# Six rows per partition set aside by SyncE instead of four, and the table's first parts fetched in between

## The chip, the cores and the metric

The kernel runs on one core of a Trainium2 chip. A core has engines that run side by side, each with its own instruction stream: TensorE (matrix products and transposes), VectorE, ScalarE, GpSimd and SyncE, and 16 DMA engines that move data between HBM and the on-chip memory (SBUF). SyncE does no arithmetic: it starts transfers. The metric is the device time in microseconds (us) from the start to the end of one execution; the median of three timed executions is given. The profile is of one further execution.

## The reference

1024 sequences of 50 item numbers each look up rows of an embedding table of 100001 rows with 128 numbers (row 0 counts as zeros). Running sums over the sequence are divided by a length, normalized over the batch, and fed through a recurrence over the 50 positions that counts threshold crossings ("spikes"). The counts times the whole table give the scores.

```python
emb = emb_table.at[0].set(0.0)
e = emb[seq]                                   # 1024 x 50 x 128
prefix = jnp.cumsum(e, axis=1)
denom = jnp.minimum(t_idx[None, :], lengths[:, None]).astype(e.dtype)
uF = prefix / denom[:, :, None]
mean = uF.mean(axis=0)
var = uF.var(axis=0)
y = (uF - mean) * lax.rsqrt(var + BN_EPS) * gamma + beta
x_seq = jnp.moveaxis(y, 1, 0)

def step(v, x):                                # TAU = 2, V_TH = 1
    v = v + (x - v) / TAU
    spike = atan_spike(v - V_TH)               # 1 where v >= V_TH
    v = v - lax.stop_gradient(spike) * V_TH
    return (v, spike)
_, spikes = lax.scan(step, v0, x_seq)
uF_out = spikes.mean(axis=0)                   # 1024 x 128
scores = uF_out @ emb.T                        # 1024 x 100001
```

The scores are 409.6 MB of float32, which have to be written to HBM.

## The kernel before

There are two stages. In the first, each of the T = 50 steps needs the embedding rows of all 1024 sequences at one position: 8 blocks (n = 0 to 7) of 128 rows, one row per partition. GpSimd brings a block with one indirect transfer (a gather). TensorE transposes the blocks and adds them up in PSUM (`pre`), in two halves of 512 sequences; VectorE scales each half into `uF` and takes its statistics, and does the recurrence with ScalarE. In the second stage the counts are multiplied with the table, part by part (a part is 1024 rows, 0.5 MB), and the scores are stored.

SyncE starts the loads: first the inputs, then the first 36 parts of the table in six groups of six, one large transfer a group (`rows` tiles, 3 MB each). Then it fetches some single rows of the table by itself, so that GpSimd has fewer gathers: block 0 of steps 44 to 47. For each partition it loads four item numbers into registers and starts four transfers of one row (512 bytes). Gathers of the other blocks stay with GpSimd. At the end of the first stage SyncE starts the stores of the scores.

```python
        for g in range(AHEAD):                          # AHEAD = 6 groups
            fetch(group(g), g * GROUP, GROUP)           # GROUP = 6 parts

        aside = {}
        for t0, many in ((T - 6, 4),):
            for t in range(t0, t0 + many):
                aside[t] = once.tile([P, P], F32, tag=f"aside{t}", name=f"aside_{t}")
            for p in range(P):
                _, items = nc.values_load_multi_w_load_instructions(
                    idx[p : p + 1, 0, t0 : t0 + many], engines=[mybir.EngineType.SP], ...)
                for j, item in enumerate(items):
                    nc.sync.dma_start(out=aside[t0 + j][p : p + 1, :], in_=table[bass.ds(item, 1), :])

        def gather(t):
            es[t] = gp.tile([P, B], F32, tag="e", name=f"e_{t}")      # two buffers
            for n in range(t in aside, NB):                           # NB = 8
                nc.gpsimd.indirect_dma_start(out=es[t][:, n * P : (n + 1) * P], in_=table, ...)
        ...
        for t in range(T):
            last = t == T - 1
            if t + 1 < T:
                gather(t + 1)
            e = es.pop(t)
            if last:
                s = ...(v >= V_TH)                      # the spikes of step 48, ahead of step 49
                nc.vector.tensor_tensor(negv, s, v, ALU.subtract)
            for h, cs in enumerate(halves):
                for k in range(0, BANK, P):             # BANK = 512
                    nc.tensor.matmul(                   # a transpose, added to pre
                        pre[h][:, k : k + P],
                        lhsT=aside[t] if h == k == 0 and t in aside else e[:, h * BANK + k : ...],
                        rhs=ident, is_transpose=True, ...)
                nc.vector.scalar_tensor_tensor(uF[:, cs], rlen[:, cs], 1.0 / (t + 1), pre[h], ...)
                nc.vector.bn_stats(bs[:, h, :], uF[:, cs])
            ...                                         # statistics, spikes of step t - 1, the new v
            if t in (T - 8, T - 6):                     # two parts of the table made ready
                prepare(q, ...)
```

(... marks cuts.) `prepare` transposes a part of the table and splits it into two summands; those of parts 0 and 1 are done in steps 42 and 44, the others in the second stage. There, stores go out on SyncE's queue, and further parts of the table are fetched on ScalarE's.

Of the kernel before, what the change touches and what calls it, by code (L numbers as in the profile page):

```python
# [12 lines left out]
F32 = mybir.dt.float32  # L13
BF16 = mybir.dt.bfloat16
F32R = mybir.dt.float32r
I32 = mybir.dt.int32
# [4 lines left out]
P = 128  # L21
# [4 lines left out]
BANK = 512  # L26
GROUP = 6
AHEAD = 6

WIDTHS = [2, 2, 2, 3, 3, 3, 3] + 12 * [6] + [4, 4]  # L30
NARROW, MIDDLE = 3, 7


@with_exitstack
def rec_kernel(
# [9 lines left out]
    nc = tc.nc  # L45
    B, T = seq.shape
    N, D = table.shape
    NB = B // P
# [22 lines left out]
    parts = -(-N // HALF)  # L71
    assert sum(WIDTHS) == parts
    rows = {}
# [6 lines left out]
    def size(q):  # L80
        return min(HALF, N - q * HALF)

    def group(g):
        at = g if g < AHEAD else AHEAD - 2 + g % 2
        r = rowp.tile([P, GROUP, HALF], F32, tag=f"rows{at}", name=f"rows_{g}")
        for k in range(GROUP):
            rows[g * GROUP + k] = r[:, k, :]
        return r

    def fetch(r, q, n):  # L90

        engine = nc.sync if q < AHEAD * GROUP else nc.scalar
        k = q % GROUP
        n = min(n, parts - q)
        whole = n - (size(q + n - 1) < HALF)
        if whole:
            engine.dma_start(
                out=r[:, k : k + whole, :],
                in_=table[q * HALF : (q + whole) * HALF, :].rearrange("(q p k) d -> p q (k d)", p=P, k=KQ),
            )  # L100
        if whole < n:
            full, rest = divmod(size(parts - 1), P)
            c1 = (parts - 1) * HALF
            r = r[:, k + whole, :].rearrange("p (k d) -> p k d", d=D)
            if full:
                engine.dma_start(
                    out=r[:, :full, :],
                    in_=table[c1 : c1 + full * P, :].rearrange("(k p) d -> p k d", p=P),
                )
            if rest:  # L110
                engine.dma_start(out=r[:rest, full, :], in_=table[c1 + full * P : N, :])
# [49 lines left out]
    with ExitStack() as ph:  # L161
        once = ph.enter_context(tc.tile_pool(name="once", bufs=1))
# [7 lines left out]
        idx = once.tile([P, NB, T], I32, tag="idx", name="idx")  # L170
# [5 lines left out]
        gb = once.tile([P, 2], F32, tag="gb", name="gb")  # L176
        nc.sync.dma_start(out=gb[:, 0:1], in_=gamma.rearrange("(d o) -> d o", o=1))
        nc.sync.dma_start(out=gb[:, 1:2], in_=beta.rearrange("(d o) -> d o", o=1))
        for g in range(AHEAD):
            fetch(group(g), g * GROUP, GROUP)  # L180

        aside = {}
        for t0, many in ((T - 6, 4),):
            for t in range(t0, t0 + many):
                aside[t] = once.tile([P, P], F32, tag=f"aside{t}", name=f"aside_{t}")
            for p in range(P):
                _, items = nc.values_load_multi_w_load_instructions(
                    idx[p : p + 1, 0, t0 : t0 + many],  # L190
                    engines=[mybir.EngineType.SP],
                    min_val=0,
                    max_val=N - 1,
                    skip_runtime_bounds_check_because="items are rows of the table; the transfer checks its own bounds",
                )
                for j, item in enumerate(items):
                    nc.sync.dma_start(out=aside[t0 + j][p : p + 1, :], in_=table[bass.ds(item, 1), :])

        es = {}

        def gather(t):
            es[t] = gp.tile([P, B], F32, tag="e", name=f"e_{t}")
            for n in range(t in aside, NB):
                nc.gpsimd.indirect_dma_start(  # L204
                    out=es[t][:, n * P : (n + 1) * P],
                    out_offset=None,
                    in_=table,
                    in_offset=bass.IndirectOffsetOnAxis(ap=idx[:, n, t : t + 1].bitcast(U32), axis=0),
                )

        make_identity(nc, ident)
        gather(0)


# [53 lines left out]
        def correct(t, l):  # L268
            for h in range(B // BANK):
                nc.tensor.matmul(  # L270
                    pre[h],
                    lhsT=l,
                    rhs=zT[:, h * BANK : (h + 1) * BANK],
                    start=t == 0,
                    stop=False,
                    skip_group_check=True,
                )
# [22 lines left out]
# [6 lines that stand above are left out]
                s = lp.tile([P, B], BF16, tag="s", name=f"s_{t - 1}")  # L306
                nc.vector.tensor_single_scalar(s, v, V_TH, ALU.is_ge)
                nc.vector.tensor_tensor(negv, s, v, ALU.subtract)
            uF = up.tile([P, B], F32, tag="uF", name=f"uF_{t}")
            bs = sp.tile([P, B // BANK, 6], F32, tag="bs", name=f"bs_{t}")  # L310
            for h, cs in enumerate(halves):
                for k in range(0, BANK, P):
                    nc.tensor.matmul(  # L313
                        pre[h][:, k : k + P],
                        lhsT=aside[t] if h == k == 0 and t in aside else e[:, h * BANK + k : h * BANK + k + P],
                        rhs=ident,
                        start=False,
                        stop=last,
                        is_transpose=True,
                        skip_group_check=True,  # L320
                    )
                nc.vector.scalar_tensor_tensor(uF[:, cs], rlen[:, cs], 1.0 / (t + 1), pre[h], ALU.max, ALU.mult)  # L322
                nc.vector.bn_stats(bs[:, h, :], uF[:, cs])  # L323
            if not last:
                correct(t + 1, l)
            else:

                counted(t - 1, s)
                count = once.tile([P, B], F32, tag="zT", name="count")
                for h, cs in enumerate(halves):  # L330
                    nc.scalar.copy(count[:, cs], sums[h])
            mv = sp.tile([P, 2], F32, tag="mv", name=f"mv_{t}")
            nc.vector.bn_aggr(mv, bs.rearrange("p h s -> p (h s)"))  # L333


            r = sp.tile([P, 1], F32, tag="r", name=f"r_{t}")
            nc.scalar.activation(r, mv[:, 1:2], AF.Sqrt, bias=eps)  # L337
            nc.scalar.activation(uF, uF, AF.Identity, bias=mv[:, 0:1], scale=-1.0)


            if t and not last:
                s = lp.tile([P, B], BF16, tag="s", name=f"s_{t - 1}")
                nc.vector.tensor_single_scalar(s, v, V_TH, ALU.is_ge)  # L343
                counted(t - 1, s)

            nc.vector.reciprocal(r, r)
            q = sp.tile([P, 1], F32, tag="q", name=f"q_{t}")
            nc.vector.tensor_mul(q, r, r)
            nc.vector.scalar_tensor_tensor(q, mv[:, 1:2], BN_EPS, q, ALU.add, ALU.mult)
            nc.vector.tensor_scalar(q, q, -0.5, 1.5, ALU.mult, ALU.add)  # L350
            a = sp.tile([P, 1], F32, tag="a", name=f"a_{t}")
            nc.vector.tensor_scalar(a, q, r, hgb[:, 0:1], ALU.mult, ALU.mult)  # L352


            def x(vt, cs):
                nc.scalar.activation(vt, uF[:, cs], AF.Identity, bias=hgb[:, 1:2], scale=a)  # L356

            def step(vt, cs):
                nc.vector.scalar_tensor_tensor(vt, negv[:, cs], -0.5, vt, ALU.mult, ALU.add)

            if not last:
                vt = vp.tile([P, B], F32, tag=f"v{t % 2}", name=f"v_{t}")
                x(vt, whole)
                if t:
                    nc.vector.tensor_tensor(negv, s, v, ALU.subtract)
                step(vt, whole)
                v = vt
                if t + 2 < T:
                    l = only(t + 2)

                if t in (T - 8, T - 6):
                    q = (t - T + 8) // 2
                    prepare(q, vp.tile([P, HALF], F32, tag="v1", name=f"pt_{q}"))
# [45 lines left out]
    q0 = 0  # L419
    to_split = WIDTHS[0]  # L420
    to_fetch = AHEAD * GROUP
# [4 lines left out]

    for c, W in enumerate(WIDTHS):

# [17 lines left out]
        q1 = q0 + W  # L446
        q2 = q1 + (WIDTHS[c + 1] if c + 1 < len(WIDTHS) else 0)

# [9 lines left out]
        for n in range(NB):  # L458
            if c == 0 and n == 0:
                continue  # L460
            pool, tag, most = turns[blocks % len(turns)]
# [23 lines left out]
            if n in (1, 4) and c >= MIDDLE and to_fetch < parts:  # L485
                g = to_fetch // GROUP
                if to_fetch % GROUP or to_split >= (g - 1) * GROUP:
                    if to_fetch % GROUP == 0:
                        r = group(g)
# [23 lines left out]
```

## Time and profile before

| | |
|---|---|
| time, median of 3 executions | 1776.19 us (1770.98 to 1776.4) |
| span of the profiled execution | 1569.9 us |
| GpSimd | 374.6 us busy, 402 instructions |
| VectorE | 940.7 us busy, 1161 instructions |
| TensorE (matrix products) | 1153.1 us busy, 4548 instructions |
| ScalarE | 630.6 us busy, 700 instructions |
| HBM read / written | 77.69 MB / 409.60 MB |

The profiled execution was about 205 us shorter than the timed ones; its inner times are used as they are.

In the profile, a row of slices cuts the span into 40 equal pieces, and a digit is the busy share in tenths. The chain of waits goes back from the last instruction to what released each step. A group of instructions is given with its line of the program, engine, operation, written and read tiles, count, then busy us and mean ns of one, then the idle time ahead of them and what ended it. PE and PEld are TensorE's products and weight loads, DVE is VectorE, ACT is ScalarE, POOL is GpSimd, SPq is SyncE's queue. The time shown for an instruction that starts a transfer is that of the start, not of the transfer.

### The profile page before, as it was taken

The numbers are of one execution on the slowest core, as the hardware profiler recorded it, in microseconds if no ns is written. First come the engines' busy times: TensorE is split into PE (matmuls) and PEld (weight loads), VectorE is DVE, ScalarE is ACT, GpSimd is POOL, SyncE is SP. The second block draws the span as 40 slices with busy tenths as digits, with TensorE's granted clock in tenths as the row PEclk, the third lists the DMA queues.
The fourth block names the chain that finished last, engine by engine and source line by source line (L and its number), as shares of the span: only waits on it lengthen the run. The fifth ranks groups of instructions, "written<-read, shape, count | busy, mean of one in ns | idle before, by whom it ended". The sixth has DMA issues, their size and how long they took to land.

```text
span 1569.9 us, 14231 instructions
## 1 busy us (share of the span) xinstructions
PE 1153.1 (73%) x4548; PEld 822.3 (52%) x4548; DVE 940.7 (60%) x1161; ACT 630.6 (40%) x700; POOL 374.6 (24%) x402
## 2 busy tenths in 40 slices
PE   4555555555556988899878788887788888788784
PEld 2222222222233766677666666666666666666563
DVE  4777777777778665576545555555555545555453
ACT  2322222222233554465444444444444444444342
POOL 6777777777775000000000000000000000000000
PEclk7555555555555999999999988999999998989998
DMA  9622222222222999999999999999999999999998
GB/s 342 245 55 53 55 54 54 54 53 54 52 53 64 399 411 420 420 393 428 425 432 427 429 428 424 418 422 424 428 413 420 415 424 429 421 423 409 394 423 354
DMA packets 54600, 488.25 MB, mean 311 GB/s; under 512 B 12443, under 2 KB 13756, under 8 KB 33276
## 3 DMA queue, kind: packets, MB, share of 16 engines
q1 hardware_dynamic: 33008, 429.03, 65.1%
q0 software_dynamic: 12672, 25.98, 6.2%
q10 hardware_dynamic: 8844, 32.33, 5.2%
q8 instruction: 36, 0.59, 0.1%
q14 instruction: 40, 0.33, 0.1%
HBM read 77.69 MB, written 409.60 MB: 310 GB/s over the span
## 4 chain that ended last, share of the span: by engine, by line
DMA 52%; POOL 17%; PE 11%; issue 9%; ACT 5%; DVE 4%; DVEq 0%; ACTq 0%; SPq 0%; POOLq 0%
DMA scores<-o 49%; POOL e L204 17%; PE po L149 9%; ACT o L473 5%; DMA e<-in_L_rec_emb_table,idx 3%; DVE o L471 2%; PE pt L119 1%; DVE bs L323 1%; DVE uF L322 0%; DVE s L343 0%; PE pre L313 0%; PE sums L281 0%; DMA idx<-in_r_seq 0%; ACT hi L141 0%; ACT pairs L141 0%
## 5 line engine op out<-in xcount | busy, mean ns | idle before, releaser
L471 DVE TENSOR_SCALAR o<-po 128x1024 f32<-128x1024 f32 x391 | 463.5, 1220 | 351.8 <-DMA scores<-o 323.4
L473 ACT ACTIVATE o<-po 128x1024 f32<-128x1024 f32 (+1 forms) x391 | 387.9, 1018 | 547.8 <-DMA scores<-o 344.9
L204 POOL DMA_INDIRECT e<-in_L_rec_emb_table,idx x396 | 373.9, 944 | 123.4 <-issue 114.6
L149 PE MATMUL po<-pairs,countB 128*128 128x512 f32 x1168 | 314.7, 415 | 67.6 <-ACT o L473 50.7
L149 PEld LDWEIGHTS po<-pairs,countB 128*128 128x128 f32 x1168 | 225.8, 198 | 132.5 <-ACT o L473 65.8
L149 PE MATMUL po<-pairs,countC 128*128 128x512 f32 x876 | 239.1, 419 | 43.6 <-ACT o L473 43.6
L313 PE MATMUL pre<-ident,e 128*128 128x128 f32 x396 | 153.1, 450 | 143.8 <-DMA e<-in_L_rec_emb_table,idx 142.2
L149 PEld LDWEIGHTS po<-pairs,countC 128*128 128x128 f32 x876 | 170.1, 200 | 89.7 <-ACT o L473 54.7
L313 PEld LDWEIGHTS pre<-ident,e 128*128 128x128 f32 x396 | 78.5, 201 | 236.1 <-DMA e<-in_L_rec_emb_table,idx 214.7
L142 DVE TENSOR_TENSOR pairs<-pt,pairs 128x1024 fp32r<-128x1024 f32 (+1 forms) x73 | 88.3, 1217 | 96.6 <-ACT pairs L141 96.5
L337 ACT ACTIVATE r<-mv,eps 128x1 f32<-128x1 f32 x50 | 14.7, 295 | 300.6 <-DVE mv L333 300.6
L322 DVE SCALAR_TENSOR_TENSOR uF<-rlen,pre 128x512 f32<-128x512 f32 x100 | 68.3, 683 | 103.8 <-PE pre L313 103.8
L119 PE MATMUL pt<-ident,rows 128*128 128x128 f32 x782 | 113.5, 293 | 8.0 <-ACT o L473 3.9
L119 PEld LDWEIGHTS pt<-ident,rows 128*128 128x128 f32 x782 | 102.6, 154 | 28.8 <-issue 10.0
L149 PE MATMUL po<-hi,countB 128*128 128x512 f32 x200 | 82.8, 414 | 18.8 <-ACT o L473 13.8
L281 PE MATMUL sums<-s,ident_h 128*128 128x512 bf16 x98 | 49.6, 608 | 60.6 <-DVE s L343 60.6
L270 PE MATMUL pre<-zT,l 128*128 128x512 f32 x100 | 78.0, 782 | 21.6 <-DVE uF L322 21.5
L149 PE MATMUL po<-lo,countB 128*128 128x512 f32 x200 | 80.4, 402 | 0.0
L141 ACT CAST pairs<-pt 128x1024 fp32r<-128x1024 f32 (+1 forms) x73 | 73.6, 1008 | 16.2 <-PE pt L119 15.9
L149 PE MATMUL po<-pairs,countA 128*128 128x512 f32 (+1 forms) x292 | 73.2, 393 | 9.1 <-ACT o L473 9.1
L149 PE MATMUL po<-hi,countC 128*128 128x512 f32 x150 | 62.7, 418 | 16.4 <-ACT o L473 16.4
L356 ACT ACTIVATE v<-uF,hgb,a 128x1024 f32<-128x1024 f32 x49 | 59.2, 1208 | 37.4 <-DVE a L352 37.4
(78 smaller groups left out, 821.1 us busy)
## 6 DMA issues: line engine op xcount, KB each, us to landing
scores<-o SPq DMA_DIRECT2D x96, 3072.0 KB
scores<-o SPq DMA_DIRECT2D x32, 1536.0 KB
rows<-in_L_rec_emb_table ACTq DMA_DIRECT2D x20, 1536.0 KB
scores<-o SPq DMA_DIRECT2D x22, 1024.0 KB
rows<-in_L_rec_emb_table SPq DMA_DIRECT2D x6, 3072.0 KB
scores<-o SPq DMA_DIRECT2D x8, 2048.0 KB
scores<-o SPq DMA_DIRECT2D x8, 1872.5 KB
aside<-in_L_rec_emb_table SPq DMA_DIRECT2D x512, 0.5 KB
```

Of the source, the lines that this page charges most:

```text
L119: nc.tensor.transpose(pt[:, k0 : k0 + kw], r[:kw, k0 : k0 + D], ident[:kw, :kw])
L141: nc.scalar.copy(vh, vp)
L142: nc.vector.tensor_tensor(vl, vp, vh.bitcast(F32), ALU.subtract)
L149: nc.tensor.matmul(po[:, :kw], lhsT=counts[n], rhs=part[:, k0 : k0 + kw], start=j == 0, stop=j == 1,)
L204: nc.gpsimd.indirect_dma_start(out=es[t][:, n * P : (n + 1) * P], out_offset=None, in_=table, in_offset=bass.IndirectOffsetOnAxis(ap=idx[: ...
L270: nc.tensor.matmul(pre[h], lhsT=l, rhs=zT[:, h * BANK : (h + 1) * BANK], start=t == 0, stop=False, skip_group_check=True,)
L281: nc.tensor.matmul(sums[h], lhsT=ident_h, rhs=s[:, h * BANK : (h + 1) * BANK], start=t == 0, stop=t == T - 2, skip_group_check=True,)
L313: nc.tensor.matmul(pre[h][:, k : k + P], lhsT=aside[t] if h == k == 0 and t in aside else e[:, h * BANK + k : h * BANK + k + P], rhs=ident ...
L322: nc.vector.scalar_tensor_tensor(uF[:, cs], rlen[:, cs], 1.0 / (t + 1), pre[h], ALU.max, ALU.mult)
L356: nc.scalar.activation(vt, uF[:, cs], AF.Identity, bias=hgb[:, 1:2], scale=a)
L471: nc.vector.tensor_scalar_mul(o[:, h0 : h0 + hw], po[:, :hw], 1.0 / T)
L473: nc.scalar.mul(o[:, h0 : h0 + hw], po[:, :hw], 1.0 / T)
```

## The change

SyncE takes over six blocks in place of four: blocks 6 and 7 of steps 46, 47 and 48, in place of block 0 of steps 44 to 47. It is to relieve GpSimd of two further gathers. To begin with the rows early, only the first group of the table's parts is fetched ahead of them; the other 30 parts are fetched one at a time, one after every fourth partition. The item numbers of the rows have a small tile and load of their own (`last3`).

```diff
+LATE = 3
...
-        for g in range(AHEAD):
-            fetch(group(g), g * GROUP, GROUP)
+        last3 = once.tile([P, 2, 4], I32, tag="last3", name="last3")
+        late = last3.rearrange("p n t -> p (n t)")[:, : 2 * LATE].rearrange("p (n t) -> p n t", t=LATE)
+        nc.sync.dma_start(out=late, in_=seq.rearrange("(n p) t -> p n t", p=P)[:, NB - 2 :, T - 1 - LATE : T - 1])
+        tiles = [group(g) for g in range(AHEAD)]
+        fetch(tiles[0], 0, GROUP)
 
         aside = {}
-        for t0, many in ((T - 6, 4),):
-            for t in range(t0, t0 + many):
-                aside[t] = once.tile([P, P], F32, tag=f"aside{t}", name=f"aside_{t}")
-            for p in range(P):
-                _, items = nc.values_load_multi_w_load_instructions(
-                    idx[p : p + 1, 0, t0 : t0 + many],
...
-                for j, item in enumerate(items):
-                    nc.sync.dma_start(out=aside[t0 + j][p : p + 1, :], in_=table[bass.ds(item, 1), :])
+        for n in (NB - 2, NB - 1):
+            for t in range(T - 1 - LATE, T - 1):
+                aside[t, n] = once.tile([P, P], F32, tag=f"aside{n}_{t}", name=f"aside_{n}_{t}")
+        ahead = GROUP
+        for p in range(P):
+            _, items = nc.values_load_multi_w_load_instructions(
+                last3.rearrange("p n t -> p (n t)")[p : p + 1, : 2 * LATE],
...
+            for r, item in zip(aside.values(), items):
+                nc.sync.dma_start(out=r[p : p + 1, :], in_=table[bass.ds(item, 1), :])
+            if p % 4 == 3 and ahead < AHEAD * GROUP:
+                fetch(tiles[ahead // GROUP], ahead, 1)
+                ahead += 1
...
-            for n in range(t in aside, NB):
+            for n in range(NB):
+                if (t, n) in aside:
+                    continue
                 nc.gpsimd.indirect_dma_start(
...
-                        lhsT=aside[t] if h == k == 0 and t in aside else e[:, h * BANK + k : h * BANK + k + P],
+                        lhsT=aside.get((t, c0 // P), e[:, c0 : c0 + P]),
```

The instruction order of VectorE and ScalarE is unchanged.

More of the change, by code (lines that the diff above doesn't have):

```diff
@@ L178, in rec_kernel @@
         nc.sync.dma_start(out=gb[:, 1:2], in_=beta.rearrange("(d o) -> d o", o=1))
-        for g in range(AHEAD):
-            fetch(group(g), g * GROUP, GROUP)
-        aside = {}
-        for t0, many in ((T - 6, 4),):
-            for t in range(t0, t0 + many):
-                aside[t] = once.tile([P, P], F32, tag=f"aside{t}", name=f"aside_{t}")
-            for p in range(P):
-                _, items = nc.values_load_multi_w_load_instructions(
-                    idx[p : p + 1, 0, t0 : t0 + many],
[L191 to L195, printed above, removed]
-                for j, item in enumerate(items):
-                    nc.sync.dma_start(out=aside[t0 + j][p : p + 1, :], in_=table[bass.ds(item, 1), :])
+        last3 = once.tile([P, 2, 4], I32, tag="last3", name="last3")
[3 more added lines that the diff above has]
+        fetch(tiles[0], 0, GROUP)
+        aside = {}
+        for n in (NB - 2, NB - 1):
[5 more added lines that the diff above has]
+                last3.rearrange("p n t -> p (n t)")[p : p + 1, : 2 * LATE],
+                engines=[mybir.EngineType.SP],
+                min_val=0,
+                max_val=N - 1,
+                skip_runtime_bounds_check_because="items are rows of the table; the transfer checks its own bounds",
+            )
+            for r, item in zip(aside.values(), items):
[3 more added lines that the diff above has]
+                ahead += 1
+        assert ahead == AHEAD * GROUP
         es = {}
@@ L312, in rec_kernel @@
                 for k in range(0, BANK, P):
+                    c0 = h * BANK + k
                     nc.tensor.matmul(
                         pre[h][:, k : k + P],
-                        lhsT=aside[t] if h == k == 0 and t in aside else e[:, h * BANK + k : h * BANK + k + P],
+                        lhsT=aside.get((t, c0 // P), e[:, c0 : c0 + P]),
                         rhs=ident,
```

## The prediction

> **What bounds the kernel now.** I read the page's slices first, then its chain of waits, then the costliest groups, and last the order of time at the seam between the two stages. The page's slices and, below them, two rows of its costliest groups:
>
> ```profile
> POOL 6777777777775000000000000000000000000000
> ...
> DMA  9622222222222999999999999999999999999998
> ...
> DMA scores<-o 49%; POOL e L204 17%; PE po L149 9%; ACT o L473 5%; DMA e<-in_L_rec_emb_table,idx 3%; DVE o L471 2%; PE pt L119 1%; DVE bs L323 1%; DVE uF L322 0%; DVE s L343 0%; PE pre L313 0%; PE sums L281 0%; DMA idx<-in_r_seq 0%; ACT hi L141 0%; ACT pairs L141 0%
> ...
> L204 POOL DMA_INDIRECT e<-in_L_rec_emb_table,idx x396 | 373.9, 944 | 123.4 <-issue 114.6
> ```
>
> One slice is 39.2 us. There are two stages. In the first 13 slices GpSimd issues gathers and the DMA engines are a fifth busy (after the initial loading); from about 507 us on GpSimd has nothing and the DMA engines are full with the stores of the scores. So the end is the length of the gather stage plus a stage that runs at the rate of the stores. The last line gives the pace of the first: 396 gathers of 944 ns, and before almost each one 0.3 us of "issue", in which GpSimd waits for nothing. The starts in the order of time are 1.248 us apart from the second (5.77 us) to the last (497.64 us): 394 x 1.2484 = 491.87. GpSimd never stops, not even in the first 55 us, when the table's parts fill the DMA engines.
>
> The change touches SyncE too. Its queue: first the rows set aside, asked for by tile (shortest, median and longest issue in ns, first and last start in us):
>
> ```profile
> L197 SPq DMA_DIRECT2D aside<-in_L_rec_emb_table x512: 224/225/7507, 38.0 to 356.3; - x171
> ```
>
> then two lines of the order of time (start, length):
>
> ```profile
> 3.83 33.42 SPq L97 DMA_DIRECT2D rows<-in_L_rec_emb_table  x6
> 339.90 16.62 SPq L197 DMA_DIRECT2D aside<-in_L_rec_emb_table  x29
> ```
>
> and its longest wait, with the total, the times and the longest one:
>
> ```profile
> SPq L158 <- ACT o L407: 150.6, 2, 150.2
> ```
>
> The six large fetches hold SyncE until 37 us, the 512 rows until 356.5 us; then it stands 150 us waiting for the first scores. 29 rows in 16.62 us are 0.573 us a row. Between starts of neighbouring rows the trace has 0.454, 0.408 and 0.408 us, and 1.02 us where the four row numbers of the next partition are loaded: 2.29 us a partition.
>
> Last the seam, from the order of time (start, length; the last bracket is what ended the idle time):
>
> ```profile
> 473.23 0.67 DVE L322 SCALAR_TENSOR_TENSOR uF<-rlen,pre 128x512 f32<-128x512 f32 x1
> 480.71 0.68 DVE L322 SCALAR_TENSOR_TENSOR uF<-rlen,pre 128x512 f32<-128x512 f32 x1
> 490.18 0.18 PEld L313 LDWEIGHTS pre<-ident,e 128*128 128x128 f32 x1 [1.05 <-DMA e<-in_L_rec_emb_table,idx]
> 490.69 0.69 DVE L322 SCALAR_TENSOR_TENSOR uF<-rlen,pre 128x512 f32<-128x512 f32 x1 [2.40 <-PE pre L313]
> 500.26 0.18 PEld L313 LDWEIGHTS pre<-ident,e 128*128 128x128 f32 x1 [1.18 <-DMA e<-in_L_rec_emb_table,idx]
> 500.77 0.69 DVE L322 SCALAR_TENSOR_TENSOR uF<-rlen,pre 128x512 f32<-128x512 f32 x1
> 506.78 27.50 SPq L158 DMA_DIRECT2D scores<-o  x16
> ```
>
> The uF lines are the second halves of steps 46, 47, 48 and 49; I use that instruction as the mark of a step. Steps 46 to 47 lie 7.48 us apart with no idle bracket: that is VectorE's own length of a step. Step 48 waited 2.40 us for its gather. Step 49 has no bracket either: VectorE came to it from one instruction after the other, at the moment at which the last gather was also there (500.26 + 0.51). From there to the first store are 6.01 us of a fixed chain.
>
> **What the Trainium skill says.** "DMA: Bandwidth & Descriptors", section "SWDGE vs HWDGE vs iDMA": on GpSimd a core in software computes the descriptors, for SyncE's queue hardware does, with a faster setup. The trace agrees for the instruction (944 ns against 225 ns), though a gather brings 128 rows and a row transfer one. The same page, "Issuing engines are not separate DMA queues": transfers of all issuers interleave on the same 16 engines and only issue time is saved. That is the case here: issue time on GpSimd is what the first stage lacks, and its DMA share is 0.20 to 0.21. The same page, "Latency and other measured facts", puts a floor of about 600 ns under loading registers from memory; the trace has 0.56 to 0.60 us for it. "Perfetto Trace Analysis", "DMA Instruction — SWDGE (GPSIMD)": the window of a gather ends with its descriptors, not with its data. The trace agrees: a gather's tile is used 2.53 us after the gather's start (487.65 to 490.18), though it shows 0.94.
>
> **The change, part by part.**
> 1. Gathers. Before, steps 44 to 47 have 7 (28); after, steps 44 and 45 have 8, and steps 46, 47 and 48 have 6. In all 394 instead of 396: 2 x 1.248 = 2.50 us less of GpSimd, whose last gather then starts at 495.15 and is there at 497.7.
> 2. What VectorE makes of it. Second halves now: step 43 at 447.82, 44 at 455.31, 45 at 465.75 (the part of the table prepared in step 44 costs it 3 us), then the marks above. After: step 44's last gather (number 360) starts at 452.71 + 2.53 + 0.51 = 455.75, 0.4 later than now. Step 45: + 10.44 = 466.2, step 46: + 7.48 = 473.7, step 47: 481.2, step 48: 488.7. Their last gathers (374, 380 and 386) start at 470.2, 477.7 and 485.2, and with 2.53, 0.51 and some 0.6 for two more transposes from the rows set aside the tiles are ready at 473.8, 481.3 and 488.8. So VectorE and GpSimd are level, 7.48 against 6 x 1.248 = 7.49 us. Step 49 on VectorE took 490.69 to 500.77 = 10.08 us without a wait, as two passes of the spikes stand ahead of it; its gathers need 498.2. VectorE is later: 488.8 + 10.08 = 498.9. The seam comes 500.8 - 498.9 = **1.9 us** earlier, of the 2.5.
> 3. SyncE. A partition now has six rows: 0.454 + 4 x 0.408 + 1.02 = 3.11 us, x 128 = 398 us. One partition in ten is 0.36 us longer now, which adds 5. 30 single parts at about 0.45 us of issue (the first large ones took 0.43 and 0.55): 14. The start moves from 38 to about 12 us, once the first group is out of the way (it landed at 15.7 now, beside others). Estimate of the end: 12 + 398 + 5 + 14 = 429 us. The rows are first wanted at 472.7. Some 44 us to spare, and stores wait for SyncE only at 505.
> 4. Parts of the table. The same bytes in 30 pieces over some 400 us rather than in 55 us. The first two, used in steps 42 and 44, are in the first group. As GpSimd kept its pace in the first 55 us, this frees nothing at the end. A part of 0.5 MB is 1.3 us of the DMA engines at the 410 GB/s of the later stage; a gather behind it may land that much later, which delays one step and not the next, as GpSimd is not held. The last part goes out by partition 119, near 400 us, well before the seam.
> 5. The store stage: the same stores, fetches, matmuls and evictions. The trace keeps its DMA share at 0.98 to 1.01. It starts 1.9 us earlier and ends so.
>
> Sum: - 1.9 us. The profiled execution spans 1569.9 us and the timed median is 1776.19; I can't tell from one trace where the 206 us between them lie. If they are in the store stage, as is likely where memory is the limit, nothing of the above moves. I subtract the 1.9 from the median: **1774.3 us**, a change of 0.1%.
>
> **Rivals.** (a) All of the gathers' 2.5 us arrive, if VectorE's step 49 can be shorter: 1773.7. For it: the margin between 498.9 and 498.2 is small. Against: the 10.08 us show no idle bracket. (b) SyncE becomes the bound. Rows of the last partition land after 472.7 if the loop needs 0.34 us a partition more than worked out, for instance because rows queue behind the 0.5 MB parts. Every us over is a us on the time: at 20% over, 512 us, the kernel is at about 1815 us. For it: one row waited 7.5 us and two of the early partitions 10 and 16 us behind the large fetches now. Against: later the loop keeps 2.29 us with no wait, and a part is only a sixth of such a fetch. (c) The gain vanishes in the store stage, if that runs to its own rhythm: 1776. For it: it is two thirds of the time, and 0.2% of it is more than the gain. Against: it begins with the first score and is full to the end.
>
> **Range and chances.** The three runs of before spread over 5.4 us, three times the effect. A range of 1767 to 1780 holds the spread about 1774 and a part of (c). Rival (b) at 5% is the one way to be slower by over 2% (35.5 us); no mechanism brings 35 us of gain, but the unexplained 206 us may lie otherwise in another measurement, and leave 2 to 3% for each side.
>
> **What would show it.** Right: 394 gathers at 1.25 us, last start near 495; uF second halves near 473.8, 481.3, 488.8, 498.9; first store near 504.9; SyncE's rows from about 7 to 430 us with a wait of 75 us after them. Wrong: rows until after 472 us, with TensorE waiting for them; gaps between gathers; a store stage whose DMA share falls below 0.98.

## The result, and the profile after

The changed kernel takes **1915.64 us** (median of 6 executions, 1910.19 to 1918.98) beside 1776.3 us for the kernel before (6 executions, 1770.98 to 1780.24): a ratio of **1.0782, 95% interval 1.0757 to 1.0807**. The prediction had 1774.3 us and a range of 1767 to 1780.

The page after, in the order in which the prediction read it: two rows of slices (one is now 47.9 us), the chain of waits, and two of the costliest groups.

```profile
POOL 6666766676630000010000000000000000000000
...
DMA  4222222222221111019999999999999999999998
...
DMA scores<-o 39%; PE po L150 8%; SPq L202 7%; ACT o L485 4%; SPq L194 4%; DVE o L483 1%; PE pt L120 0%; SPq L98 0%; ACT pairs L142 0%; DVE bs L335 0%; DVE uF L334 0%; DVE v L371 0%; ACT v L368 0%; DVE pairs L143 0%; DVE s L355 0%
...
L215 POOL DMA_INDIRECT e<-in_L_rec_emb_table,idx x394 | 372.2, 945 | 463.8 <-PE pre L325 277.9
...
L325 PE MATMUL pre<-ident,aside 128*128 128x128 f32 x6 | 2.2, 427 | 274.4 <-DMA aside<-in_L_rec_emb_table 274.4
```

GpSimd, which had been without a pause for 13 slices, is idle from slice 13 to 17 and then issues its last gathers. In the chain its 17% are gone, and SyncE's row transfers (L202) and register loads (L194) stand there with 11%. The last line says what was waited for: TensorE stood 274.4 us in front of a tile whose rows SyncE fetches. Those rows by tile (columns as in the prediction; below them, the idle time ahead of their users, and who waited, in us and times; the 549.5 us count one wait twice, 275.1 for TensorE's weight loads and 274.4 for its products):

```profile
L202 SPq DMA_DIRECT2D aside<-in_L_rec_emb_table x768: 2/228/1396, 7.5 to 821.4; - x192
...
  DMA aside<-in_L_rec_emb_table: 549.5, 4
...
  POOL e L215: 273.3, 1
  DVE uF L334: 272.9, 1
```

They end at 821.4 us, not at 429. The order of time at that place, with what ended each idle time:

```profile
820.64 0.18 PEld L325 LDWEIGHTS pre<-ident,aside 128*128 128x128 f32 x1 [274.07 <-DMA aside<-in_L_rec_emb_table]
...
822.33 0.69 DVE L334 SCALAR_TENSOR_TENSOR uF<-rlen,pre 128x512 f32<-128x512 f32 x1 [272.87 <-PE pre L325]
...
827.70 0.95 POOL L215 DMA_INDIRECT e<-in_L_rec_emb_table,idx  x1 [273.28 <-PE pre L325]
```

Everything hangs on the rows of step 46: TensorE's transpose, VectorE's `uF`, and GpSimd, whose next buffer is freed by the transposes of step 47, which stand behind that one on TensorE. SyncE's longest wait for the first scores, 150 us in the profile before, has shrunk to 31:

```profile
SPq L159 <- ACT o L419: 33.1, 3, 31.4
```

The last view gives three stretches (start and end, length, busy us of PE, PEld, DVE, ACT and POOL with counts, then TensorE's clock, DMA share, GB/s):

```profile
40.00:553.00 513.00, 190.48 (x552) 115.50 (x551) 320.80 (x585) 130.94 (x182) 339.45 (x360) 0.60 0.23 60
553.00:821.00 268.00, 0.33 (x1) 0.18 (x1) 0.00 (x0) 0.00 (x0) 1.11 (x2) 0.50 0.11 35
853.00:1917.00 1064.00, 887.66 (x3899) 696.50 (x3898) 577.46 (x492) 479.41 (x490) 0.00 (x0) 0.94 0.99 416
```

For 268 us next to nothing runs but SyncE. The store stage from the first store at 853.1 takes 1064.0 us, where it took 1063.1 before (506.8 to 1569.9). It is blameless.

That is rival (b), SyncE as the bound, but far beyond its size. Two questions follow. Why 821 us for a loop worked out at 429? And where did the kernel before have its 206 us, the difference between 1569.9 profiled and 1776.19 timed?

### The profile page after: what moved, and what is told of

Read it like the earlier page. It is cut to its first block, busy times and chain, and to the rows that moved or that the text cites. A ratio compares the mean times of both kernels' runs of the same rounds, so it can differ in the third digit from the quotient of the medians.

```text
span 1917.1 us, 15027 instructions
## 1 busy us (share of the span) xinstructions
PE 1108.9 (58%) x4548; PEld 831.8 (43%) x4548; DVE 940.3 (49%) x1161; ACT 630.7 (33%) x700; POOL 372.9 (19%) x400
## 4 chain that ended last, share of the span: by engine, by line
DMA 39%; SPq 11%; PE 8%; ACT 4%; issue 4%; DVE 3%; ACTq 0%; DVEq 0%
DMA scores<-o 39%; PE po L150 8%; SPq L202 7%; ACT o L485 4%; SPq L194 4%; DVE o L483 1%; PE pt L120 0%; SPq L98 0%; ACT pairs L142 0%; DVE bs L335 0%; DVE uF L334 0%; DVE v L371 0%; ACT v L368 0%; DVE pairs L143 0%; DVE s L355 0%
## 5 line engine op out<-in xcount | busy, mean ns | idle before, releaser
L281 PE MATMUL pre<-zT,l 128*128 128x512 f32 x100 | 72.5, 727 | 273.0 <-DVE uF L334 220.9
L281 PEld LDWEIGHTS pre<-zT,l 128*128 128x128 f32 x100 | 26.9, 271 | 313.1 <-issue 217.5
L325 PE MATMUL pre<-ident,aside 128*128 128x128 f32 x6 | 2.2, 427 | 274.4 <-DMA aside<-in_L_rec_emb_table 274.4
L325 PEld LDWEIGHTS pre<-ident,aside 128*128 128x128 f32 x6 | 1.2, 211 | 275.1 <-DMA aside<-in_L_rec_emb_table 275.1
L325 PE MATMUL pre<-ident,e 128*128 128x128 f32 x394 | 96.4, 419 | 5.1 <-DMA e<-in_L_rec_emb_table,idx 3.1
L325 PEld LDWEIGHTS pre<-ident,e 128*128 128x128 f32 x394 | 85.1, 226 | 30.1 <-issue 25.1
```

Of the source, the lines that this page charges most:

```text
L281: nc.tensor.matmul(pre[h], lhsT=l, rhs=zT[:, h * BANK : (h + 1) * BANK], start=t == 0, stop=False, skip_group_check=True,)
L325: nc.tensor.matmul(pre[h][:, k : k + P], lhsT=aside.get((t, c0 // P), e[:, c0 : c0 + P]), rhs=ident, start=False, stop=last, is_transpose= ...
```

## The experiments

The theories at the start: **A**, SyncE's loop runs at a third of its pace while GpSimd issues gathers, so that in the timed executions of before, too, the rows came late. Against it, the single parts of the table hold up the rows (**C**), or the register load is larger than I took it. Whatever the letters, each expectation below says what it expects.

### Where the kernel before has its 206 us

`before_again` is the kernel before, unchanged, with a profile of the chip on which it takes 1776 us.

> The kernel before, looked at once more, unchanged. Theory A: SyncE's row loop is what ends last in the first stage whenever its instructions fall into a slow pace (0.7 us each) beside the gathers; then the 206 us between the timed 1776 us and the profiled 1570 us lie in that loop, and this look shows a row loop that ends near 700 us instead of 356 us, TensorE waiting for a row tile at step 44, and a store stage as long as before (1063 us). Rival B: the 206 us lie in the store stage (slower memory): row loop done by 360 us, store stage 1270 us.

1779.5 us (one execution, beside 1776.28 for 8 of the same). The rows by tile, and the first store:

```profile
L197 SPq DMA_DIRECT2D aside<-in_L_rec_emb_table x512: 2/225/7535, 37.8 to 656.7; - x171
...
  DMA aside<-in_L_rec_emb_table: 134.1, 1
...
713.52 1.23 SPq L158 DMA_DIRECT2D scores<-o  x2
```

The rows end at 656.7 us, where the profile that I predicted from had 356.3; TensorE waits 134.1 us for them in step 44. The first store is at 713.5, and the store stage takes 1064.2 us. So the 206 us lie in the gather stage: it is 206.7 us longer (713.5 - 506.8), of the 207.8 us by which this span exceeds that of the profile before (1777.7 - 1569.9). The kernel before was already bound by SyncE in the executions that were timed, and the profile which I had showed an execution in which it was not.

`no_rows` leaves the rows to GpSimd: the kernel before, with 400 gathers.

```diff
-        for t0, many in ((T - 6, 4),):
-            ...                                  # the whole loop of rows
         aside = {}
```

> The kernel before with no rows fetched by SyncE at all: all 400 gathers on GpSimd, the six groups of the table fetched as before. Theory A: the seam is set by the gathers alone, 400 x 1.248 us, that is 5 us later than in the profiled execution of before, so 1575 to 1580 us, about 0.89 of before. Rival B: the timed executions are long in the store stage, so 1781 us, 1.003 of before.

1644.9 us, ratio 0.9261 [0.9231, 0.9292]: this beats both kernels here. But it is 65 to 70 us more than expected. The gathers by line, and what ended the idle time ahead of them:

```profile
L191 POOL DMA_INDIRECT e<-in_L_rec_emb_table,idx x400: 941/947/1168, 4.0 to 562.7; - x134
...
  remote: 59.5, 18
```

400 gathers 1.248 us apart would start up to 503; here the last starts at 562.7, as GpSimd stops 19 times (starts over 1.8 us apart), 59.1 us beyond its pace in all, for something that the trace gives no name ("remote"). Each stop stands ahead of the first gather of a step, the one that needs a free buffer, while a gather itself takes 947 ns as before. So it is not SyncE alone that is held: the buffers come back late too.

### The parts in between, and fewer rows

`parts_first` is the changed kernel with all six groups fetched ahead of the rows, as before.

```diff
-        fetch(tiles[0], 0, GROUP)
+        for g in range(AHEAD):
+            fetch(tiles[g], g * GROUP, GROUP)
...
-            if p % 4 == 3 and ahead < AHEAD * GROUP:
-                ...
```

> The changed kernel with all six groups of the table fetched in large transfers ahead of the rows, six rows a partition as changed. Theory A (the loop is slow because it runs beside the gathers, wherever the parts are): still far above 1776, 1850 to 1950 us, with a row loop that ends after 750 us. Rival C (the single parts between the rows slow the loop and hold the semaphores): row loop at 3.5 us a partition from 38 us, done near 490 us, and a time of 1590 to 1600 us.

1921.87 us, 1.0818 [1.0782, 1.0854]; rows until 824.3. The parts in between cost nothing, C falls, and the earlier start of the rows (7.5 instead of 38 us) brings 3 us at the end: what is done early is done at the slow pace.

`late2` is the changed kernel with four rows a partition, of steps 47 and 48 (396 gathers).

```diff
-LATE = 3
+LATE = 2
```

> The changed kernel with four rows a partition (blocks 6 and 7 of steps 47 and 48) in place of six, single parts in between as changed. Theory A, cost by the row: two thirds of the rows, so the loop ends about 250 us earlier than 821 us if its slow pace is by instruction, a time between 1640 and 1780 us, near that of before, which has as many rows. Rival C (the parts in between): the 30 parts are still there, so most of the 140 us over before stays, 1850 us or more.

1762.04 us, 0.9920 [0.9894, 0.9947]. Rows until 675.9, first store at 701.1. The number of rows decides.

The pace can be read from the starts of the row transfers, cut at the point where GpSimd issues no more gathers:

| kernel | us a row beside gathers | us a row once GpSimd has stopped |
|---|---|---|
| before_again | 1.71 (285 rows) | 0.58 (227) |
| after | 1.65 (332) | 0.61 (436) |
| parts_first | 1.64 (314) | 0.60 (454) |
| late2 | 1.69 (333) | 0.60 (179) |

That settles A, and the size of the loss: the change has 256 rows more. 47 of them find room beside the gathers (332 - 285), as the rows begin 30 us earlier and GpSimd goes on 30 us longer, to 554.4 instead of 524.4. The other 209 come when GpSimd has stopped, 209 x 0.61 = 128 us; the 227 rows that before too has left take 0.03 us more each, 7 us. 30 + 128 + 7 = 165 us, and the rows do end 164.7 us later (821.4 - 656.7). Of these, 25 us come back: after the last row there are two steps fewer to do (853.1 - 821.4 = 31.7 us to the first store, against 713.5 - 656.7 = 56.8). 164.7 - 25.1 = 139.6 us, and 139.3 were measured (1915.64 - 1776.3).

### What is held beside the gathers

A stretch of the order of time of the changed kernel:

```profile
172.01 18.90 SPq L202 DMA_DIRECT2D aside<-in_L_rec_emb_table  x12
...
174.25 1.91 PE L325 MATMUL pre<-ident,e 128*128 128x128 f32 x8
...
181.59 0.94 POOL L215 DMA_INDIRECT e<-in_L_rec_emb_table,idx  x1 [0.30 <-issue]
186.80 0.69 DVE L334 SCALAR_TENSOR_TENSOR uF<-rlen,pre 128x512 f32<-128x512 f32 x1 [9.88 <-remote]
187.17 0.94 POOL L215 DMA_INDIRECT e<-in_L_rec_emb_table,idx  x1 [4.64 <-remote]
```

Twelve rows take 18.90 us. VectorE's `uF` waits 9.88 us, though the eight transposes which it needs are recorded as ended at 176.2. GpSimd pauses from 182.5; 4 us later SyncE, VectorE and then GpSimd go on. In such stretches nearly every instruction of SyncE takes about 0.70 us, even the register moves, which wait for nothing and take 0.03 us otherwise.

The hold builds up while gathers run without a stop. Of GpSimd's 22 short pauses in this trace, 17 are followed by over 19 us of gathers. In the first 3 us of these, SyncE starts 15.3 instructions on average, which is its undisturbed pace (15.6 in 3 us, in `after_again` below); from 6 to 9 us it starts 6.0, and from 15 to 18 us 2.5. Four kernels ask what makes it so.

`few_gathers`: the changed kernel with the gathers of three of four steps left out (those steps use old rows, so that its output is not the scores).

```diff
         def gather(t):
+            if t % 4:
+                es[t] = held[-1]
+                return
             es[t] = gp.tile([P, B], F32, tag="e", name=f"e_{t}")
+            held.append(es[t])
```

> The changed kernel with the gathers of three steps in four left out (the steps use the tile of the last step that has them; the output is not the scores wanted). The 768 rows and the single parts stay. Theory A (SyncE's instructions are slow because GpSimd's gathers run beside them): the loop keeps 3.5 us a partition from early on and ends near 480 us instead of 821 us; first store near 520 us, time 1580 to 1600 us. Rival D (the loop is slow by itself or because the other engines' steps run beside it): it stays at some 1.75 us a row until the steps reach the rows, and ends after 650 us; 1750 us or more.

1627.89 us, 0.9157 [0.9137, 0.9176]:

```profile
L202 SPq DMA_DIRECT2D aside<-in_L_rec_emb_table x768: 2/228/1385, 7.5 to 530.6; - x192
```

0.72 us a row up to GpSimd's last gather, instead of 1.65. With the gathers most of the slowness goes; a SyncE that is slow whatever GpSimd does falls. The end at 530.6 is 50 us later than expected. The median partition does take the 3.5 us expected (3.56), but the 478 rows beside the few gathers cost 0.72 us each and not 0.61, which makes these 50 us.

`const_rows`: the row numbers are fixed, so that SyncE loads no register and adds nothing (the rows are not those asked for, and the output is not the scores). The same 768 transfers.

```diff
-            _, items = nc.values_load_multi_w_load_instructions(...)
-            for r, item in zip(aside.values(), items):
-                nc.sync.dma_start(out=r[p : p + 1, :], in_=table[bass.ds(item, 1), :])
+            for j, r in enumerate(aside.values()):
+                nc.sync.dma_start(out=r[p : p + 1, :], in_=table[128 * j + p + 1 : 128 * j + p + 2, :])
```

> The changed kernel with the rows' numbers fixed in the program: no loading of registers and no arithmetic on them, 768 row transfers as before, of the same size, from other rows of the table (the output is not the scores wanted). SyncE then has one instruction a row in place of about 3.2. Theory A1 (in the slow stretches each instruction of SyncE costs some 0.7 us, whatever it is): a third of the time, 0.55 us a row, so the rows end before 460 us, nothing waits for them, time 1635 to 1660 us. Rival A2 (the cost is by the transfer): 1.7 us a row remain, the rows end after 750 us, 1850 us or more.

1650.94 us, 0.9286 [0.9266, 0.9306]:

```profile
L195 SPq DMA_DIRECT2D aside<-in_L_rec_emb_table x768: 2/251/1435, 4.6 to 517.4; - x192
```

0.67 us a row beside all the gathers (0.55 expected), 0.64 us for each of SyncE's instructions; in the changed kernel a row is some 3.2 instructions at 0.51. So it is the instructions that are held, not the transfers: as many transfers of the same size are started by 517 us if there is one instruction to each.

`late1`: two rows a partition, of step 48 (`LATE = 1`).

> The changed kernel with two rows a partition (blocks 6 and 7 of step 48 only). Theory A: 256 rows at 1.75 us end before 520 us, step 48 wants them at some 548 us, so nothing waits; the time is that of no rows at all less two gathers of 1.25 us and plus what the rows cost the gathers: 1640 to 1655 us. Rival C (the parts in between): 30 parts stay and with them most of the 140 us over before, above 1780 us.

1653.74 us, 0.9302 [0.9286, 0.9317]. Rows until 539.0, and nothing waits for them; first store at 588.5. 2.09 us a row here, as a register load falls on two rows instead of six.

`three_bufs`: no_rows with a third buffer for the gathered rows, in case GpSimd's pauses are waits for a free one.

```diff
-        gp = ph.enter_context(tc.tile_pool(name="gather", bufs=2))
+        gp = ph.enter_context(tc.tile_pool(name="gather", bufs=3))
```

> The kernel before without rows, with three buffers for gathered steps in place of two. In the look at no rows GpSimd stood still 21 times for 60 us in all, each time until a buffer came free. Theory A (the others are held while GpSimd runs on, and freed when it has to stop): it stops once in three or four steps in place of two or three, and less in all, 35 to 50 us: 1620 to 1640 us. Rival F (the other engines are simply slower than the gathers, 11.25 us a step, and buffers don't matter): within 3 us of no rows, 1642 to 1648 us.

1652.85 us, 0.9296 [0.9281, 0.9312], no better than no_rows and outside both expectations, though nearer to rival F; the pauses stay: 18, 60.7 us in all. More room for the gathers takes nothing away.

So on the chips used up to here the gathers bring the hold on, and it is paid by the instruction. Which path is held stays open. One candidate is untested: the recording of the instructions itself. Each execution here, the timed ones too, has its span and clock on record, and the traces of the slower kind lack most records of gathers landing (last section).

### The other kind of chip

`three_rows` keeps block 7 only (three rows a partition, 397 gathers); `halves` is no_rows with buffers for 512 sequences instead of 1024, so that GpSimd is freed sooner.

```diff
-        for n in (NB - 2, NB - 1):
+        for n in (NB - 1,):
```

```diff
-            es[t] = gp.tile([P, B], F32, tag="e", name=f"e_{t}")
+            es[t] = [gh.tile([P, BANK], F32, tag=f"e{h}", name=f"eh{h}_{t}") for h in range(B // BANK)]
```

> The changed kernel with three rows a partition (block 7 of steps 46, 47 and 48). By the count that the looks so far give, 0.50 us for each of SyncE's instructions while gathers run and about 0.60 us a row after they have stopped: 3.4 instructions a row make 1.72 us, so some 320 of the 384 rows are out by 557 us, when GpSimd has to stop for them; 64 more end near 597 us, the first store comes near 630 us, time 1697 us (1680 to 1710). Rival: nothing is lost until all of GpSimd's time is used up, so as with two rows, 1650 to 1660 us.

> The kernel before without rows, with one buffer for each half of a gathered step (four blocks), so that GpSimd is at most one step ahead and not two. Theory G (the longer GpSimd may run on without a stop, the more the others are held; a third buffer cost 8 us): its stops become shorter and more frequent and the gather stage shorter, 1620 to 1642 us. Rival H (the room only decides where the waiting happens): GpSimd has to wait for the transposes at every half step and the stage gets longer, 1650 to 1700 us.

1573.64 us (1.0010 [1.0003, 1.0017]) and 1579.90 us (1.0048 [1.0031, 1.0065]): both far from what was expected, because the kernel before now took 1572.23 us (1571.65 to 1572.79 in 23 executions). This was another chip. That is the plain fact behind the 206 us: on some chips the kernel before takes 1768 to 1781 us in every execution, on others 1570 to 1573, and the profile that I predicted from was of the second kind, the times of the first. I call them held and free chips, though it may be a condition of the chip at the time (last section). (What both kernels ask about a held chip stays unanswered; neither was seen on one.)

Four kernels on a free chip, where before takes 1571.27 us (18 executions):

> The changed kernel once more, unchanged, beside the kernel before on the same chip. In the last study the kernel before took 1572 us in each of 23 executions on one chip, on three others 1776. Theory A': the slow pace of SyncE beside the gathers is a condition of the chip and not of the kernel. Where before takes 1572 us, the changed kernel then does what its instruction counts say: SyncE's loop at 3.5 us a partition ends near 470 us, the seam comes 1 to 2.5 us earlier, 1569.5 to 1572 us, ratio 0.998 to 1.000. Where before takes 1776 us, it takes 1915 us again, ratio 1.078. Rival J: six rows are too many in either case (the loop ends after 472 us even at its fast pace): above 1580 us where before takes 1572.

> The kernel before without rows, once more. Theory A': where before takes 1572 us, four more gathers of 1.25 us make 1577 us, ratio 1.003. Where before takes 1776 us, 1645 us again, ratio 0.926. Rival: rows never help, so below before in both cases.

> Three rows a partition once more. Where before takes 1572 us, 1573.6 us again. Where before takes 1776 us, the expectation of the first look stands: SyncE at 0.50 us an instruction, 1697 us (1680 to 1710). Rival: as with two rows, 1650 to 1660 us.

> No rows, one buffer for each half of a gathered step, once more. Where before takes 1572 us, 1580 us again. Where before takes 1776 us, the expectations of the first look stand: theory G (less run-ahead, shorter holds) 1620 to 1642 us, rival H (more waiting) 1650 to 1700 us.

| kernel | us | ratio |
|---|---|---|
| after_again (the changed kernel) | 1580.43 | 1.0057 [1.0044, 1.0071] |
| no_rows_again | 1576.78 | 1.0034 [1.0021, 1.0047] |
| three_rows_again | 1572.58 | 1.0008 [0.9999, 1.0017] |
| halves_again | 1579.29 | 1.0055 [1.0039, 1.0070] |

On the free chip the changed kernel loses 9 us instead of 139, and the kernel without rows, 131 us better than the kernel before on the held one, loses 5.5. Its gathers no longer pause:

```profile
L191 POOL DMA_INDIRECT e<-in_L_rec_emb_table,idx x400: 941/947/1168, 4.0 to 503.3; - x134
```

For the changed kernel, the rows by tile:

```profile
L202 SPq DMA_DIRECT2D aside<-in_L_rec_emb_table x768: 224/228/328, 7.7 to 482.6; - x192
```

and the seam in the order of time:

```profile
469.02 0.67 DVE L334 SCALAR_TENSOR_TENSOR uF<-rlen,pre 128x512 f32<-128x512 f32 x1
...
481.86 0.18 PEld L325 LDWEIGHTS pre<-ident,aside 128*128 128x128 f32 x1 [7.88 <-DMA aside<-in_L_rec_emb_table]
...
491.08 0.67 DVE L334 SCALAR_TENSOR_TENSOR uF<-rlen,pre 128x512 f32<-128x512 f32 x1
...
514.89 5.23 SPq L159 DMA_DIRECT2D scores<-o  x5
```

No row transfer is above 328 ns now (1396 on the held chip), TensorE waits 7.88 us in place of 274, and the first store goes out at 514.9. The loop still ends at 482.6 and not at 429: the second error, without the first. That is rival J of after_again. A' had 3.5 us a partition and an end near 470; with the single parts in between it is 3.72 on average. The register loads by line, min, median and longest in ns:

```profile
L194 SPq TENSOR_LOAD <-last x128: 907/991/1165, 6.5 to 479.3; - x128
```

0.99 us for six numbers, where I had carried over the 0.56 to 0.60 us of four.

### The register load by itself

`three_rows` had loads of three numbers of 0.945 us, so the duration does not go by the count. `eight_loads` loads eight numbers a partition, a whole row of `last3`, and uses six of them; `after_beside` is the changed kernel again, on the same free chip. (The 0.7 us of two numbers in the expectation below comes from late1, on a held chip, where almost any instruction takes that.)

```diff
-        late = last3.rearrange("p n t -> p (n t)")[:, : 2 * LATE].rearrange("p (n t) -> p n t", t=LATE)
-        nc.sync.dma_start(out=late, in_=seq.rearrange(...)[:, NB - 2 :, T - 1 - LATE : T - 1])
+        late = last3
+        nc.sync.dma_start(out=late, in_=seq.rearrange(...)[:, NB - 2 :, T - 1 - LATE :])
...
-                last3.rearrange("p n t -> p (n t)")[p : p + 1, : 2 * LATE],
+                last3.rearrange("p n t -> p (n t)")[p : p + 1, :],
...
-            for r, item in zip(aside.values(), items):
+            for r, item in zip(aside.values(), items[:LATE] + items[LATE + 1 : 2 * LATE + 1]):
```

> The changed kernel with eight numbers loaded in place of six for each partition (the two of step 49 besides, which are not used); the rows fetched are the same six. A load of four numbers took 0.56 us, of six 0.99, of three 0.94, of two 0.7. Theory K (a load of a power of two of numbers is one short access, of others it isn't): 0.6 us again, 3.1 us a partition, the loop ends near 430 us and nothing waits for it: where before takes 1572 us, 1569 to 1571 us. Rival L (the cost grows with the numbers loaded): 1.1 us or more, 3.7 us a partition, the loop ends near 495 us, 1590 us. Where before takes 1776 us both give 1900 to 1920 us, since there a load costs the same as any instruction.

> The changed kernel, unchanged, on the same chip: 1580 us where before takes 1572, 1915 us where before takes 1776.

eight_loads: 1569.54 us, 0.9990 [0.9981, 0.9998]; after_beside: 1581.63 us, 1.0062 [1.0047, 1.0078]; before 1571.35 us in 17 executions. The loads of eight_loads, then its rows:

```profile
L194 SPq TENSOR_LOAD <-last x128: 712/792/959, 6.2 to 454.4; - x128
```

```profile
L202 SPq DMA_DIRECT2D aside<-in_L_rec_emb_table x768: 224/228/328, 7.2 to 457.5; - x192
```

Eight numbers load in 0.79 us, 0.2 us less than six; neither theory had that duration, though the time is the one that K expected. A partition takes 3.36 us, the loop ends at 457.5, 25 us earlier than with six (128 x 0.2), and no transpose waits for a row. VectorE's marks, the second halves of steps 46 to 49:

```profile
473.66 0.69 DVE L334 SCALAR_TENSOR_TENSOR uF<-rlen,pre 128x512 f32<-128x512 f32 x1
...
481.16 0.67 DVE L334 SCALAR_TENSOR_TENSOR uF<-rlen,pre 128x512 f32<-128x512 f32 x1
...
488.65 0.67 DVE L334 SCALAR_TENSOR_TENSOR uF<-rlen,pre 128x512 f32<-128x512 f32 x1
...
498.66 0.67 DVE L334 SCALAR_TENSOR_TENSOR uF<-rlen,pre 128x512 f32<-128x512 f32 x1
```

This is the execution that the prediction describes, but for the end of the loop (429 there). It beats both kernels on a free chip, by 1.8 and 12 us; on a held one it was not seen. no_rows beats both on a held chip and not on a free one. No run shows a version that beats both on both.

## Why the prediction was wrong, step by step

**Part 1, gathers: right** where nothing waits. In eight_loads the last gather starts at 495.0 (predicted 495.15).

**Part 2, VectorE: right.** Predicted marks 473.7, 481.2, 488.7 to 488.8 and 498.9; eight_loads has 473.66, 481.16, 488.65 and 498.66. The predicted gain of 1.9 us was measured as 1.8 (1571.35 - 1569.54).

**Part 3, SyncE: wrong, twice over.** First the register load: "0.454 + 4 x 0.408 + 1.02 = 3.11 us" took the load of four numbers for one of six. It is 0.99 us and not 0.56, the partition takes 3.56 us, and the free chip alone shows what that is worth: 128 x 0.43 = 55 us, an end at 482.6 us and not 429, 9.9 us after the rows are wanted at 472.7. Rival (b) had the threshold at 0.34 us a partition, and 0.43 passes it; its "every us over is a us on the time" holds too: the first store is 10.0 us later than predicted (514.9 against 504.9), and the time 11.1 us above the 1569.4 that the gain of 1.9 would have left of 1571.27. The Trainium skill's floor of about 600 ns, in "DMA: Bandwidth & Descriptors", section "Latency and other measured facts", gives no duration for a count: the loads here took 0.56 us for four numbers, slightly under it, 0.79 for eight, 0.945 for three and 0.99 for six. The start, on the other hand, was better than the 12 us worked out: the first row went out at 7.7 us.

Second, and 15 times as large: the pace was read from one execution and taken for that of the timed ones. On a held chip a row costs 1.65 us beside gathers, not 0.4 to 0.6, and for 268 us all other engines wait. Rival (b)'s own case against itself, "later the loop keeps 2.29 us with no wait", was true of the profile only.

**Part 4, parts in between: right.** With the parts first the time is no better (1921.87 us against 1915.64).

**Part 5, store stage: right.** 1064.0 us against 1063.1, and between 1062.7 and 1065.1 in all 18 traces.

**The sum: the failing step.** "If they are in the store stage, as is likely where memory is the limit, nothing of the above moves." All but 1 us of the difference between profile and timed executions lay in the gather stage (before_again), in the very loop that the change makes half as long again. The store stage spoke against this guess already: it filled the DMA engines at 0.98 to 1.01 for 1063 us and moved a fixed number of bytes, so that 206 us more of it would have meant a rate a sixth lower, for which nothing in the profile spoke. The gather stage had a loop of hundreds of short instructions with 94.5 us to spare (its rows were out at 356.5 us and first used at 451.0), and nothing said that the spare time was there in the timed executions. The 5% for rival (b) came of taking it to be so.

## What to carry to other kernels

Where a profile and the timed runs differ by a tenth, put the difference down to a stage before working out any change: take each stage's length from the profile, and ask which of them could hold it. A long run of short instructions with operands in registers on one engine is the least sure thing in a sum; give each kind of it its own measured duration, and do not carry a register load's time from one count of numbers to another. And try a change on more than one chip: no_rows is 7.4% faster on one kind and 0.3% slower on the other.

## What the runs showed of the hardware

- **Two kinds of chips.** The kernel before took 1776 to 1778 us in the first result and on two chips of the experiments, and 1571 to 1572 on three others (medians; no execution of one kind came near the other). Each chip was seen at one time only. The held chips all ran earlier than the three free ones, though the profile that I predicted from, which is older than all of these, is of the free kind; whether the chip itself or its condition at the time makes the kind isn't told apart.
- **What a held chip does.** Beside indirect gathers SyncE's instructions start 0.51 to 0.64 us apart on average (0.19 in the changed kernel once GpSimd has stopped), GpSimd pauses 18 to 26 times for 59 to 69 us in all, each time ahead of the first gather of a step, and VectorE waits up to 12 us (before_again) for transposes that are recorded as ended. (few_gathers, with its short runs of gathers, is left out here.) Of the steps by which gathers report that they have landed, the trace of the changed kernel has 903 of 6304 on a held chip and 6287 on a free one. The nine traces of held chips have a fifth of them at most, the nine of free chips over 99%: the two go together in all 18, but that one causes the other isn't shown.
- **Register loads** do not grow with the count: 0.56 us for four numbers (from the small tile in late2 as from the large one before), 0.79 for eight, but 0.945 for three and 0.99 for six. A reason isn't shown.
